# Window attention on one core: group-norm squares one per step, and 3x3 taps of the late strips shared out anew between VectorE, GpSimd and the routing

## The chip, the core and the metric

The kernel runs as one program on one core of one Trainium2 chip. The metric is the device time of one execution in microseconds. Before the change it was 12002.51 us, the median of three runs (11993.68 to 12006.19).

The core has five engines, each with its own instruction stream, which it works off in the order in which the program wrote it: TensorE (PE in the profile: matmuls and transposes into PSUM), VectorE (DVE), ScalarE (ACT), GpSimd (POOL), and SyncE (SP), which only issues transfers. They meet at semaphores: an instruction waits until what it reads has been written and what it overwrites has been read.

## The reference, cut to what matters

Four images of 256 channels and 64x64 pixels go through four layers; each is `x = x + layer(group_norm(x))`. Layers 0 and 1 are the ones the change is in: a two-way scan over the rows (computed by 1x1 convolutions, tanh, and a linear recurrence), then window attention with a 3x3 depthwise convolution of the values ("lepe") added to the attention's result. Layers 2 and 3 are state-space layers ("mamba"); they are not touched.

```python
def _gn(v, G=32, eps=1e-5):                  # one mean and variance per group of 2 columns
    m = jnp.mean(g, axis=(1, 2, 4), keepdims=True)
    s = jnp.var(g, axis=(1, 2, 4), keepdims=True)
    return ((g - m) / jnp.sqrt(s + eps)).reshape(v.shape)
...
def ssa(x_img, qkv_w, qkv_b, wo_w, wo_b, lepe_w, lepe_b):
    qkv = xw @ qkv_w.T + qkv_b               # 64 windows of 8x8 pixels
    logit = jnp.einsum('bpc,bqc->bpq', q_win * SCALE, k_win)
    tk_logit, idx = jax.lax.top_k(logit, TOPK)        # each window attends to 4 windows
    attn = jax.nn.softmax(jnp.einsum('bphqd,bphkd->bphqk', qh * SCALE, kh), axis=-1)
    out = jnp.einsum('bphqk,bphkd->bphqd', attn, vh)
    lepe = conv_general_dilated(v_img, lepe_w, (1, 1), 'SAME', feature_group_count=C) + lepe_b
    out_img = out_img + lepe
    return out_img @ wo_w.T + wo_b
```

## The kernel before, in words

An image stays in on-chip memory as `x`, 128 partitions by two channel halves by 4096 pixels. It is cut into 8 **strips** of 8 columns; a strip holds 4 groups of the group norm and one column of 8 windows. Per image the program does: attention layer 0, attention layer 1, then the two mamba layers. An attention layer has three stages.

**Scan stage** (`scan_phase`). One round per strip s: convolutions, the scan, and then `keys_values(s - 1)`, which makes keys and values of the strip before it (the values also as an image, `vimg`, line 357) and stores them in `kv_dram` for later gathers. Each round also runs the 3x3 taps of strip s-3 (`lepe`), so that strips 0 to 4 are done when the rounds end. After the last round comes `keys_values(7)`.

**Routing stage** (`routing` and the lines after its call). Means of queries and keys per window, logits, the four largest: a short chain that ends in the index list `idx`. Behind it stand the query convolutions of strips 2 to 4 on TensorE, evicted by VectorE, with the taps of strip 5 between them: channel half m=0 on VectorE, m=1 on GpSimd.

**Pair stage** (`window_phase`). 32 steps, i = 0 to 31, two windows each; strip sj = i // 4, and a = i % 4 is the place in the strip. A step is software pipelined with its neighbours and in two head halves h: scores on TensorE (line 538), their minimum on VectorE (`smallest`, line 550), exponentials with row sums on ScalarE (`exps`, line 561), a reciprocal on VectorE (line 573), four multiplications by it on GpSimd (`normalise`, line 576), transposes on TensorE (`turn`, line 589), copies out of PSUM by VectorE and ScalarE (`turned`, lines 600 and 602), products with the values (`values`, line 615), and the addition to `vimg` on VectorE (`own_rows`, line 626). Steps with a = 1 and 2 (from strip 1 on) also project the strip before (`project`: four 512-column matmuls, line 232, and an addition to `x` on VectorE, line 636). Steps 19, 20, 23 and 24 have a query convolution instead.

Every engine's order is written out by hand. Within a step there are two places where other work is hung in: **mids**, after the third and fourth exponential and ahead of `normalise(i, 0)`, and **ends**, after everything else of the step. A dictionary names for each step what goes there.

- **The taps.** A 3x3 convolution of one strip and channel half is nine taps. On VectorE a tap is one instruction (line 268 for the first, 270 for the others); in the scan and routing stages it accumulates in PSUM (`lp`), in the pair stage in `vimg` itself. On GpSimd the first tap is one instruction and each of the others two, `weigh` (line 253, into a scratch tile) and `add` (line 256): 17 pieces per half strip. The scratch tile has the tag "sq" of pool `norm`, with one buffer, and the group norm of the next layer (`gn`) takes the same tag for its squares. In the pair stage GpSimd has 51 pieces, one after each `normalise`, in steps 0 to 25: half m=1 of strip 6, then both halves of strip 7. VectorE has half m=0 of strip 6, one tap in each of steps 2 to 10.
- **Group norm for the next layer.** In layer 0's pair stage the strips 0 and 1 of `x` are normalised for layer 1 (`gn`): sums, a matmul that averages over partitions, `center` on GpSimd (line 151), a square on ScalarE (line 156), a reduction on VectorE (line 160), the matmul again, and `scale` on GpSimd (lines 168 and 172). In layer 1's pair stage all strips but the last get only their statistics for layer 2 (`stats`): sums on VectorE (line 200), the matmul (line 195), the mean (line 206), **squares**, four instructions on ScalarE in a row (line 215), the matmul, the variance (line 221). The two matmuls write the PSUM tile "mm", of which the pair stage has one, and which the convolutions use too.

What is left over when the 32 steps end (`left`) runs with the last projections.

Of the kernel before, what the change touches and what calls it, by code (L numbers as in the profile page):

```python
# [8 lines left out]
F32 = mybir.dt.float32  # L9
BF16 = mybir.dt.bfloat16  # L10
U32 = mybir.dt.uint32
AF = mybir.ActivationFunctionType
# [6 lines left out]
P = 128  # L19
NB = 4  # L20
C = 256
S = 64
T = S * S
NW = 8
# [20 lines left out]
class Net:  # L45
# [33 lines left out]
    def attention_layers(self, x, w_drams, v_drams):  # L79
        tc, nc = self.tc, self.nc  # L80
        with ExitStack() as ctx:
# [107 lines left out]
            def stats(s, psum):  # L189
                xs = x.rearrange("p (c h w) -> p c w h", c=2, w=S)[:, :, strip[s], :]  # L190
                box = {}
# [17 lines left out]

                def squares():  # L210
                    box["s2"] = self.small.tile([P, 4], F32, tag="gn_s2", name="gn_s2")
                    sq = norm.tile([P, 2, 8, S], F32, tag="xn", name="gn_sq")
                    for g in range(4):
                        two = slice(2 * g, 2 * g + 2)
                        nc.scalar.activation(
                            sq[:, :, two], xs[:, :, two], AF.Square,
                            bias=box["mean"][:, g : g + 1], accum_out=box["s2"][:, g : g + 1],
                        )

                def variance():  # L220
                    nc.vector.tensor_copy(self.gvar[:, 4 * s : 4 * s + 4], box["pv"][:, 0:4])

                return (
                    sums, lambda: columns("pm", box["s1"]), mean, squares,
                    lambda: columns("pv", box["s2"]), variance,
# [91 lines left out]
            def scan_phase(lay, work, psum, tail):  # L317
# [78 lines left out]
                for s in range(NW):  # L396
# [32 lines left out]
                    if s in (5, 6):  # L429
                        for evict in [query(lay, s - 5, m, psum) for m in range(2)]:  # L430
                            evict()
                keys_values(NW - 1)


# [33 lines left out]

            def window_phase(lay, work, psum, idx, nxt):
                vec, wb = lay["vec"], lay["wb"]  # L470
# [181 lines left out]
                smallest(0, 1)  # L652
                taps6, taps7 = (lepe(lay, s, pool=True) for s in (NW - 2, NW - 1))
                taps = taps6[17:] + taps7[17:] + taps7[:17]
                dve_taps = lepe(lay, NW - 2)[:9]

# [9 lines left out]
                if nxt:  # L666
                    load_scan_weights(nxt)
                    for s in range(2):
                        i = 10 + s
                        plan(gn(nxt, s, lambda: psum), (ends, i), (ends, i + 1), (mids, i + 2),  # L670
                             (ends, i + 2), (mids, i + 3), (ends, i + 5), (mids, i + 6))
                else:

                    for s in range(NW - 1):
                        i = 4 * s + 6
                        last = i + 6 if s < 5 else i + 3
                        plan(stats(s, lambda: psum), (ends, i), (ends, i + 1), (mids, i + 2),
                             (ends, i + 2), (ends, last), (mids, last + 1))
                for i in range(n_pair):
                    sj, a = divmod(i, 4)  # L680
# [14 lines left out]
                    normalise(i, 0)  # L695
                    for t in taps[2 * i : 2 * i + 1]:
                        t()
                    if a == 3 and sj + 2 in (NW - 2, NW - 1):
# [15 lines left out]
                    if i:  # L714
                        own_rows(i - 1)
                    for t in taps[2 * i + 1 : 2 * i + 2]:
                        t()
                    for t in dve_taps[i - 2 : i - 1] if i > 1 else ():
                        t()
                    if add:  # L720
# [36 lines left out]
            for i, lay in enumerate(layers):  # L757
                with tc.tile_pool(name=f"at_a{i}", bufs=1, reuse_waits="tile") as work, tc.tile_pool(
                    name=f"at_p{i}", bufs=5, space=PSUM, reuse_waits="tile"
                ) as psum:  # L760
                    box["psum"] = psum
                    scan_phase(lay, work, psum, tail)
                    idx = routing(lay, work, psum)
                    taps = lepe(lay, NW - 3, psum)[:9]
                    for s in range(2, 5):
                        evicts = [query(lay, s, m, psum, nc.vector) for m in range(2)]
                        for t in taps[3 * s - 6 : 3 * s - 3]:
                            t()
                        for evict in evicts:
                            evict()  # L770
                    for t in lepe(lay, NW - 3, pool=True)[17:]:
                        t()
                with tc.tile_pool(name=f"at_c{i}", bufs=1, reuse_waits="tile") as work, tc.tile_pool(
                    name=f"at_q{i}", bufs=1, space=PSUM, reuse_waits="tile"
                ) as psum:
                    nxt = layers[i + 1] if i + 1 < len(layers) else None
                    box, tail, left = window_phase(lay, work, psum, idx, nxt)
                    if nxt is None:
                        box["psum"] = psum
                        g = stats(NW - 1, lambda: psum)  # L780
                        for t in (left[0], tail[0], left[1], tail[1], g[0], left[2], left[3], *g[1:]):
                            t()
# [1381 lines left out]
```

## Time and profile before

| what | value |
|---|---|
| median of three runs | 12002.51 us |
| the profiled execution: its own time | 11985.03 us |
| its span, first to last instruction | 11983.3 us |
| PE, DVE, ACT, POOL busy | 84%, 82%, 58%, 74% of the span |
| pair stage, layer 0, first image: first exponential to last of step 31 | 234.6 to 487.5 us |
| pair stage, layer 1, first image | 701.2 to 954.1 us |
| granted TensorE clock, whole span | 0.932 |
| granted TensorE clock, the two pair stages | 0.92 and 0.91 |

The profile is one execution on the chip with the start and length of each instruction. A group row gives an engine, an operation, the tiles it writes and reads, how many there are, busy time, the mean length of one, and the idle time just before them with what ended it. A row of the timeline gives start, length, engine, line and operation; in square brackets stands how long the engine had been idle and who released it. A windows row gives, for a stretch of time, each engine's busy time and the share of its full clock that TensorE was granted. A step of the pair stage is measured here from its first exponential (line 561) to that of the next step; there are eight per step. There are eight pair stages, two per image, and the four images' stages differ little from each other: layer 0's last from 244.7 to 249.6 us and layer 1's from 246.4 to 248.6 us, first exponential of step 0 to first exponential of step 31.

### The profile page before, as it was taken

Reading aid. Unit: us, or ns where it says so; the run is one execution under the profiler, and the core shown is the slowest. Engines: PE = TensorE matmul, PEld = TensorE weight load, DVE = VectorE, ACT = ScalarE, POOL = GpSimd, SP = SyncE. Lnnn points to the kernel's source line nnn. Section 1 sums busy time; section 2 is a strip of 40 time slices with the busy share of each in tenths; the row PEclk is TensorE's granted clock in tenths of the full one; section 3 lists DMA queues with packets and bytes.
Section 4 is the critical chain, followed back from the end, with each engine's and each line's share of the span. In section 5 each row is a group of like instructions: output and inputs, shape, how many; then the busy total and the mean of one; then the engine's idle time right before and its main releaser. Section 6 shows DMA issues by size and latency. Waiting matters only on the chain.

```text
span 11983.3 us, 192241 instructions
## 1 busy us (share of the span) xinstructions
PE 10083.2 (84%) x71104; PEld 5778.2 (48%) x71104; DVE 9833.8 (82%) x8350; ACT 7002.3 (58%) x13096; POOL 8811.5 (74%) x6054
## 2 busy tenths in 40 slices
PE   8998887777899888777799988877778998887777
PEld 4564554444455455444445645544444554554444
DVE  6677998998666799899866779989986667998998
ACT  4555555776455555477645555547764555554776
POOL 4666886898456688689745668868984666887897
PEclk9999998999999899899999989989999999998999
DMA  3343454454334355445433434444543343454454
GB/s 96 100 126 134 174 175 149 169 180 160 92 98 127 134 173 177 145 169 182 159 90 99 128 132 173 174 148 167 180 160 91 100 127 135 173 176 146 169 176 154
DMA packets 682506, 1742.10 MB, mean 145 GB/s; under 512 B 88896, under 2 KB 194896, under 8 KB 681312
## 3 DMA queue, kind: packets, MB, share of 16 engines
q1 hardware_dynamic: 676448, 1721.41, 43.1%
q10 hardware_dynamic: 5120, 8.39, 0.3%
q8 instruction: 563, 9.22, 0.3%
q14 instruction: 375, 3.07, 0.1%
HBM read 1601.52 MB, written 94.39 MB: 142 GB/s over the span
## 4 chain that ended last, share of the span: by engine, by line
DVE 23%; PE 23%; ACT 8%; issue 5%; POOL 4%; DMA 1%; SPq 0%; DVEq 0%; POOLq 0%; ACTq 0%
DVE h L1002 13%; DVE pb L996 5%; PE conv_ps L232 4%; PE y L954 4%; PE u_ps L1291 3%; ACT da L938 2%; PE pb L926 1%; PE u_ps L1664 1%; POOL pr L576 1%; PE sc L538 1%; DVE lp L270 1%; PE pt_ps L589 1%; ACT dap L938 1%; PE z_ps L1316 1%; POOL hc L1008 1%
## 5 line engine op out<-in xcount | busy, mean ns | idle before, releaser
L1008 POOL TENSOR_TENSOR hc<-h,cb 128x1024 f32<-128x1024 f32 x2056 | 4809.6, 2350 | 806.4 <-DVE h L1002 350.9
L1002 DVE TENSOR_TENSOR_SCAN h<-da,m_state,pb 128x1024 f32<-128x1024 f32 x1248 | 2920.6, 2340 | 161.4 <-DVE pb L996 2.4
L954 PE MATMUL y<-ident,hc 128*128 128x128 f32 x16384 | 2333.6, 290 | 408.0 <-POOL hc L1008 340.9
L954 PEld LDWEIGHTS y<-ident,hc 128*128 128x128 f32 x16384 | 2034.5, 150 | 1124.9 <-POOL hc L1008 577.0
L996 DVE TENSOR_TENSOR pb<-du,pb 128x1024 f32<-128x1024 f32 x1672 | 2025.4, 1211 | 113.4 <-PE pb L926 110.9
L938 ACT ACTIVATE da<-delta,m_v 128x1024 f32<-128x1024 f32 x1672 | 1899.5, 1141 | 135.5 <-DVE h L1002 118.3
L926 PE MATMUL pb<-m_parts,pick 128*128 128x512 bf16 x3312 | 1078.2, 410 | 846.1 <-DVE h L1002 777.6
L576 POOL TENSOR_SCALAR pr<-pr,sm,zero 128x256 f32<-128x256 f32 x2048 | 1136.5, 569 | 476.8 <-DVE sm L573 475.8
L561 ACT ACTIVATE pr<-sc,mn 128x256 f32<-128x256 f32 x2048 | 955.9, 482 | 647.5 <-DVE sm L573 480.9
L926 PEld LDWEIGHTS <-pick 128*128 128x128 bf16 x3312 | 263.1, 101 | 1787.4 <-DVE h L1002 981.2
L550 DVE TENSOR_REDUCE mn<-sc 128x4 f32<-128x1024 f32 x512 | 627.9, 1228 | 550.0 <-PE sc L538 547.2
L1002 DVE TENSOR_TENSOR_SCAN h<-da,pb 128x1024 f32<-128x1024 f32 x424 | 969.5, 2287 | 55.1 <-DVE pb L996 0.9
L912 POOL TENSOR_TENSOR bb<-du,bb 128x1024 f32<-128x1024 f32 x376 | 888.6, 2363 | 88.8 <-DMA bb<-m_cd 84.0
L589 PE MATMUL pt_ps<-ident,pr 128*128 128x128 f32 x4096 | 705.4, 304 | 144.3 <-POOL pr L576 51.1
L1002 DVE TENSOR_TENSOR_SCAN h<-dap,m_state,bb 128x1024 f32<-128x1024 f32 x288 | 672.4, 2335 | 65.1 <-ACT dap L938 45.9
L232 PE MATMUL conv_ps<-att_y,att_wb 128*128 128x512 f32 x1536 | 683.3, 594 | 1.3 <-DVE gn_mean L206 1.3
L589 PEld LDWEIGHTS pt_ps<-ident,pr 128*128 128x128 f32 x4096 | 490.3, 151 | 307.5 <-POOL pr L576 161.7
L538 PE MATMUL sc<-kv,q_swap 32*64 32x128 f32 x8192 | 597.2, 287 | 6.7 <-DMA kv<-kv_dram 4.7
L938 ACT ACTIVATE dap<-delta,m_v 128x1024 f32<-128x1024 f32 x376 | 419.7, 1116 | 304.0 <-DVE h L1002 234.2
L538 PE MATMUL sc<-kv,att_y 32*64 32x128 f32 x7168 | 569.2, 287 | 11.8 <-DMA kv<-kv_dram 7.5
L538 PEld LDWEIGHTS sc<-kv,att_y 32*64 32x64 f32 x7168 | 430.0, 139 | 144.9 <-ACT pr L561 65.6
L270 DVE SCALAR_TENSOR_TENSOR lp<-vimg,att_v,lp 128x512 f32<-128x512 f32 x616 | 465.4, 756 | 28.1 <-DVE lp L270 1.4
(300 smaller groups left out, 17937.9 us busy)
## 6 DMA issues: line engine op xcount, KB each, us to landing
cb<-m_cd SPq DMA_DIRECT2D x2048, 512.0 KB, 3.8
kv<-kv_dram SPq DMA_DIRECT2D x1984, 128.0 KB, 2.8
bb<-m_cd SPq DMA_DIRECT2D x376, 512.0 KB, 5.4
kv_dram<-kst SPq DMA_DIRECT2D x128, 256.0 KB
kv_dram<-vn SPq DMA_DIRECT2D x128, 256.0 KB, 4.1
q_swap<-att_y SPq DMA_DIRECT2D x96, 256.0 KB, 4.3
m_pe<-in_pe_dram SPq DMA_DIRECT2D x32, 512.0 KB, 4.1
out_dram<-yo SPq DMA_DIRECT2D x64, 256.0 KB, 2.4
```

The lines of the kernel that those rows point to most:

```text
L232: nc.tensor.matmul(ps, w[:, k, w0 + m * P : w0 + (m + 1) * P], src[:, k], start=(k == 0), stop=(k == 1),)
L538: nc.tensor.matmul(sc[h][b * 64 : b * 64 + 64, r, w, m, :], (own(sj, m) if r == b else swap[sj % 2][:, m])[rows, 2 * a + w], kv[i, w][rows ...
L561: nc.scalar.activation(t[:, g].rearrange("p j r t -> p r j t"), sc[h][:, :, g // 2, g % 2, :].rearrange("p r (j t) -> p r j t", j=2), AF.E ...
L576: nc.gpsimd.tensor_scalar(t[:, g], t[:, g], s[:, g : g + 1], self.zero, ALU.mult, ALU.add)
L589: nc.tensor.transpose(pt[h][j][:, g, :], t[:, g, j].rearrange("p r t -> p (r t)"), self.ident,)
L912: nc.gpsimd.tensor_tensor(pb[i], slots[i][0]["du"], pb[i], ALU.mult)
L926: nc.tensor.matmul(pb[i][:, ss], self.pick[:, n : n + 1].to_broadcast([P, P]), blk["parts"][:, ss], start=True, stop=True,)
L938: nc.scalar.activation(da[i], blk["delta"], AF.Exp, scale=blk["a"](n))
L954: nc.tensor.matmul(blk["y"][:, ss], t[:, ss], self.ident, is_transpose=True, start=(n == 0 and ss.start % NT == 0), stop=(n == DS - 1 and ...
L996: nc.vector.tensor_tensor(pb[i], blk["du"], pb[i], ALU.mult)
L1002: nc.vector.tensor_tensor_scan(h[i][:, ss], da[i][:, ss], pb[i][:, ss], state, ALU.mult, ALU.add)
L1008: nc.gpsimd.tensor_tensor(hc[i][:, ss], h[i][:, ss], cb[i][:, ss], ALU.mult)
```

## The change

1. **Squares one by one.** `squares`, which issued four ScalarE instructions, becomes `square(g)`, which issues one; the plan puts them at four places.
2. **Other places in the plan.** In layer 1, `stats` of strip s starts at step i = 4s + 7 (before, 4s + 6): sums at the end of step i, matmul at the end of i+1, mean in the middle of i+2, the four squares at the end of i+2, middle of i+3, end of i+3, middle of i+4, the second matmul at the end of i+4, the variance in the middle of i+5. In layer 0, `gn` of strips 0 and 1 starts at steps 7 and 11 (before, 10 and 11): sums end of i, mean matmul end of i+1, `center` middle of i+2, square end of i+3, reduction middle of i+4, matmul end of i+4, `scale` middle of i+5.
3. **Taps of strip 5 ahead of `keys_values(7)`.** Half m=0 on VectorE (nine taps) and the first 5 of the 17 GpSimd pieces of half m=1 come before it, the other 12 pieces after it.
4. **Taps of strip 6 in the routing stage.** Half m=0 on VectorE between the queries, where strip 5 was, and 9 of the 17 GpSimd pieces of half m=1.
5. **Taps in the pair stage.** GpSimd has 25 pieces: 8 of strip 6 and the 17 of strip 7's half m=1, one at the end of each of steps 0 to 24. VectorE has half m=0 of strip 7, at the end of steps 3, 4, 7, 8, 11, 12, 15, 16 and 19.
6. **The last steps of layer 1** are reordered to match: the statistics of strip 6 now begin at step 31 and end among the last projections.

```diff
-                def squares():
-                    box["s2"] = self.small.tile([P, 4], F32, tag="gn_s2", name="gn_s2")
-                    sq = norm.tile([P, 2, 8, S], F32, tag="xn", name="gn_sq")
-                    for g in range(4):
-                        two = slice(2 * g, 2 * g + 2)
-                        nc.scalar.activation(
-                            sq[:, :, two], xs[:, :, two], AF.Square,
-                            bias=box["mean"][:, g : g + 1], accum_out=box["s2"][:, g : g + 1],
-                        )
+                def square(g):
+                    if g == 0:
+                        box["s2"] = self.small.tile([P, 4], F32, tag="gn_s2", name="gn_s2")
+                        box["sq"] = norm.tile([P, 2, 8, S], F32, tag="xn", name="gn_sq")
+                    two = slice(2 * g, 2 * g + 2)
+                    nc.scalar.activation(
+                        box["sq"][:, :, two], xs[:, :, two], AF.Square,
+                        bias=box["mean"][:, g : g + 1], accum_out=box["s2"][:, g : g + 1],
+                    )
...
                 return (
-                    sums, lambda: columns("pm", box["s1"]), mean, squares,
+                    sums, lambda: columns("pm", box["s1"]), mean,
+                    *(lambda g=g: square(g) for g in range(4)),
                     lambda: columns("pv", box["s2"]), variance,
                 )
...
+                for t in lepe(lay, NW - 3, psum)[:9]:
+                    t()
+                later = lepe(lay, NW - 3, pool=True)[17:]
+                for t in later[:5]:
+                    t()
                 keys_values(NW - 1)
+                for t in later[5:]:
+                    t()
...
-                taps6, taps7 = (lepe(lay, s, pool=True) for s in (NW - 2, NW - 1))
-                taps = taps6[17:] + taps7[17:] + taps7[:17]
-                dve_taps = lepe(lay, NW - 2)[:9]
+                taps = taps + lepe(lay, NW - 1, pool=True)[17:]
+                dve_taps = lepe(lay, NW - 1)[:9]
...
                     for s in range(2):
-                        i = 10 + s
+                        i = 7 + 4 * s
                         plan(gn(nxt, s, lambda: psum), (ends, i), (ends, i + 1), (mids, i + 2),
-                             (ends, i + 2), (mids, i + 3), (ends, i + 5), (mids, i + 6))
+                             (ends, i + 3), (mids, i + 4), (ends, i + 4), (mids, i + 5))
                 else:
 
                     for s in range(NW - 1):
-                        i = 4 * s + 6
-                        last = i + 6 if s < 5 else i + 3
+                        i = 4 * s + 7
                         plan(stats(s, lambda: psum), (ends, i), (ends, i + 1), (mids, i + 2),
-                             (ends, i + 2), (ends, last), (mids, last + 1))
+                             (ends, i + 2), (mids, i + 3), (ends, i + 3), (mids, i + 4),
+                             (ends, i + 4), (mids, i + 5))
...
                     normalise(i, 0)
-                    for t in taps[2 * i : 2 * i + 1]:
-                        t()
...
-                    for t in taps[2 * i + 1 : 2 * i + 2]:
+                    for t in taps[i : i + 1]:
                         t()
-                    for t in dve_taps[i - 2 : i - 1] if i > 1 else ():
-                        t()
+                    if a in (0, 3) and i and dve_taps:
+                        dve_taps.pop(0)()
...
                     idx = routing(lay, work, psum)
-                    taps = lepe(lay, NW - 3, psum)[:9]
+                    taps = lepe(lay, NW - 2, psum)[:9]
...
-                    for t in lepe(lay, NW - 3, pool=True)[17:]:
+                    later = lepe(lay, NW - 2, pool=True)[17:]
+                    for t in later[:9]:
                         t()
...
-                    box, tail, left = window_phase(lay, work, psum, idx, nxt)
+                    box, tail, left = window_phase(lay, work, psum, idx, nxt, later[9:])
                     if nxt is None:
                         box["psum"] = psum
                         g = stats(NW - 1, lambda: psum)
-                        for t in (left[0], tail[0], left[1], tail[1], g[0], left[2], left[3], *g[1:]):
+                        var, left = left[0], left[1:]
+                        for t in (var, tail[0], left[0], left[1], tail[1], *left[2:6], g[0],
+                                  left[6], left[7], *g[1:]):
                             t()
```

## The prediction, made before the changed kernel was run

> **What bounds the kernel now.** I read the page first, then windows of single steps and groups of steps, then timelines of ScalarE, GpSimd and VectorE in them.
>
> ```profile
> span 11983.3 us, 192241 instructions
> PE 10083.2 (84%) x71104; PEld 5778.2 (48%) x71104; DVE 9833.8 (82%) x8350; ACT 7002.3 (58%) x13096; POOL 8811.5 (74%) x6054
> DVE h L1002 13%; DVE pb L996 5%; PE conv_ps L232 4%; PE y L954 4%; PE u_ps L1291 3%; ACT da L938 2%; PE pb L926 1%; PE u_ps L1664 1%; POOL pr L576 1%; PE sc L538 1%; DVE lp L270 1%; PE pt_ps L589 1%; ACT dap L938 1%; PE z_ps L1316 1%; POOL hc L1008 1%
> ```
>
> No engine bounds the whole. Most of the chain (L1002, L996) is the mamba layers, which stay as they are. What can move is the eight pair stages, some 255 us each, 17% of the span. There the question is what a step costs with and without other work:
>
> ```profile
> 409.80:417.00 7.20, 7.06 (x151) 4.99 (x150) 4.15 (x9) 4.83 (x18) 6.22 (x10) 1.00 0.49 148
> 289.00:295.50 6.50, 5.50 (x139) 4.02 (x138) 6.03 (x8) 4.65 (x18) 5.51 (x10) 1.00 0.52 164
> 760.10:771.77 11.67, 11.67 (x187) 10.32 (x180) 6.09 (x12) 7.82 (x28) 9.11 (x14) 0.50 0.34 100
> 326.40:341.30 14.90, 12.82 (x228) 10.33 (x220) 7.92 (x13) 6.00 (x22) 12.72 (x17) 0.73 0.48 141
> 373.10:386.90 13.80, 11.40 (x166) 8.19 (x155) 4.49 (x10) 5.01 (x21) 12.80 (x16) 0.75 0.43 128
> ```
>
> Columns: length, busy time of PE, weight loads, DVE, ACT, POOL, then the granted clock. Row one is step 21, with a projection: TensorE is busy 7.06 of 7.20, it sets the step. Row two is step 7 of layer 0, without a projection but with a VectorE tap: 6.5. The other three are steps with group-norm work: step 8 of layer 1 (squares) and steps 12 and 17 of layer 0 (`center`, `scale`). They are 5 to 8 us longer and at a lower clock. What happens in them:
>
> ```profile
> 768.81 0.80 ACT L215 ACTIVATE gn_sq<-x,gn_mean 128x256 f32<-128x256 f32 x1
> 771.05 0.75 ACT L215 ACTIVATE gn_sq<-x,gn_mean 128x256 f32<-128x256 f32 x1
> ...
> 340.29 1.06 ACT L156 ACTIVATE gn_sq<-att_xn 128x1024 f32<-128x1024 f32 x1 [6.34 <-POOL vimg L256]
> ```
> ```profile
> 331.60 2.48 POOL L151 TENSOR_TENSOR att_xn<-x,gn_mean 128x1024 f32<-128x1024 f32 x1 [1.14 <-DVE sm L573]
> 334.05 2.17 POOL L576 TENSOR_SCALAR pr<-pr,sm,zero 128x256 f32<-128x256 f32 x4
> 336.19 0.77 POOL L253 TENSOR_SCALAR tap<-vimg,att_v,zero 128x512 f32<-128x512 f32 x1
> ```
>
> Layer 1: the first and last of four squares; from 768.81 to 771.8 ScalarE does nothing else, and the exponentials of step 9 stand behind it: 3.0 us. Layer 0: the square needs the scratch tile "sq", so it waits for the tap's `add` (L256) at the end of GpSimd's queue, itself behind `center`: ScalarE stands 6.34 us.
>
> **Part 1, squares one by one (layer 1).** In a step set by TensorE, ScalarE has two holes:
>
> ```profile
> 398.78 0.47 ACT L561 ACTIVATE pr<-sc,mn 128x256 f32<-128x256 f32 x1 [0.99 <-DVE sm L573]
> 409.82 0.47 ACT L561 ACTIVATE pr<-sc,mn 128x256 f32<-128x256 f32 x1 [1.14 <-DVE sm L573]
> ```
>
> 0.99 us at mids; 1.14 at ends, even behind a query eviction of 0.71. A square takes a place of 0.75, so each of the four fits and costs nothing; if the hole were gone it would cost 0.75. The block's 3.0 us per strip go. What comes instead: the mean (0.15, behind a 1.22 minimum) now stands ahead of the projection's matmuls, which need the one "mm" tile: TensorE waits about 0.5 (the variance did this in steps 13, 17, 21, 25, so there it is no news). Sums (1.22) stand at the end of steps with a = 3, behind a tap up to step 19, and delay `turned` by 0.8; before, they stood behind tap and addition. From step 23 on nothing is lost: own rows and sums are 0.4 + 1.22, as much as own rows and an addition (0.4 + 1.36).
>
> Layer 1, by groups of four steps (first image). After: a = 1 7.7 (with the mean), a = 2 7.3, a = 3 6.6 (6.9 with the second matmul), a = 0 7.4 (6.6 and the sums' 0.8):
> - steps 5 to 8: 35.8 now; 7.2 + 7.2 + 6.6 + 7.4 = 28.4
> - 9 to 12: 32.8; 7.7 + 7.3 + 6.9 + 7.4 = 29.3
> - 13 to 16: 33.3; 29.3
> - 17 to 20: 30.9; two query steps, 7.7 + 7.3 + 7.5 + 8.4 = 30.9
> - 21 to 24: 30.9; 7.7 + 7.3 + 7.3 + 7.9 = 30.2
> - 25 to 28: 30.9; 7.7 + 7.3 + 6.8 + 7.0 = 28.8
> - 29 and 30: 17.0; 7.7 + 7.3 = 15.0
>
> 211.6 becomes 191.9, less 19.7. The tail pays: sums of strip 6 in the last step (half hidden, +0.6) and its matmul between the two last projections (+0.6): net 18.5 per image.
>
> **Part 2, the norm of layer 0.** `center` (2.48) is still ahead of `normalise(i, 0)`; a transpose needs that 1.1 us after it ends (GpSimd's multiplications end at 401.03 in step 19, its transposes start about 402.2), less with the tap gone, so it costs 1.7 (bounds 1.4 and 2.5). `scale` is 1.65 + 1.90 by the trace, less the same 1.1: 2.5. The square stands at the end of steps 10 and 14, where the piece before it is again an `add` (pieces 9 to 24 alternate). That `add` waits for `normalise(i, 1)`, whose reciprocal comes late: in the trace step 19 starts at 395.38 and step 18's multiplications run to 397.65, so the `add` would end at 398.8, 3.4 us after the next step's exponentials are due. Cost 3.4, between 2 (GpSimd ahead) and 4.5 (the square's own 1.06 added), plus 1.0 for clock: 4.4. Layer 0, steps 4 to 19: 136.8 now. After: 4 and 7 at 6.6; 5, 6, 10, 14, 17, 18 at 7.3; 8 at 7.4; 9 and 13 at 9.0; 11 and 15 at 11.0; 12 at 9.9 (with the second sums); 16 at 9.1; 19 at 7.5. Sum 130.9, less 5.9. Steps 1 to 3 wait for the first gathers and stay.
>
> **Part 3, taps moved ahead of and around the routing.** The hole they go into:
>
> ```profile
> 217.81 0.69 DVE L389 COPY vn<-vt_ps 128x512 f32<-128x512 f32 x1 [7.10 <-PE vt_ps L383]
> 212.99 0.67 POOL L361 COPY vst<-vimg 128x512 f32<-128x512 f32 x1 [5.12 <-ACT vimg L357]
> 238.37 2.16 POOL L576 TENSOR_SCALAR pr<-pr,sm,zero 128x256 f32<-128x256 f32 x4 [5.36 <-DVE sm L573]
> ```
>
> VectorE is idle 7.10 us before the last `vn` copy; the round before, nine PSUM taps ran from 184.47 to 191.67, 7.2. The copy comes 0.1 late; ScalarE's half of `vn` ends later still (218.84), so nothing follows. GpSimd is idle 5.12: five pieces are 0.77 + 2 x 2.13 (start to start in a lone row of pieces) = 5.0. The other 12 (12.8) and 9 of strip 6 (9.3) start at 215.3 and end at 237.4; `normalise(0, 0)` starts at 238.37 (0.5 us of room in layer 1). Cost 0, cover gone: 1 us per layer. The half strip that changes engine is 16.4 us of GpSimd pieces against 7.2 of VectorE.
>
> [...] Row: taps that accumulate in `vimg` took 969 ns (median), in PSUM 756 ns, also beside GpSimd pieces. [...] The nine pair-stage taps are as many as before.
>
> **Part 4, fewer pieces in the pair stage.** GpSimd loses 26 of 51 pieces, some 25 us per layer, but where TensorE sets the step that is idle time. It pays in steps 5, 6, 9, 10 (8.7, 7.9, 8.4, 7.9 in layer 0, to 7.3), which is in the sums above. No transfer and no ScalarE or SyncE queue entry moves; GpSimd issues none.
>
> **Sum.** 18.5 + 5.9 = 24.4 per image, 97.6 in four. The profiled execution took 11985.03 (span plus 1.7); less 97.6 is 11887. The median stands 17.5 above it, so I predict **11905**.
>
> [...] In the pair stages 8% and 9% of the clock is missing, 20 to 23 us each if all were on the path; I book none of it as gain beyond the sums.
>
> **Rivals.**
> - *More* (0.14): the clock stays full once the blocks are gone and the square waits are short; layer 1 gives 24, layer 0 14: 38 per image, 11850. For it: groups 17 to 24 already run at 1.00.
> - *Less* (0.16): steps without a projection are held by their hand-offs, not by squares; each square shifts a minimum or a transpose. Layer 1 gives 9, layer 0 nothing: 11966.
> - *No change* (0.04): the saved time turns into waits for gathers. Against it: gathers are issued three steps ahead, TensorE waits for `kv` before step 4 and then only at step 28, under 0.7 us.
> - *Slower* (0.06), by the clock: where one long stall per strip shut the gate once, small gaps in three steps shut it three times. A 3.4 us window at half clock costs 1.7; the pair stages lose (1 - clock) x 255. To eat the 24.4 per image the clock must fall by 0.05 in both, to 0.87 and 0.86; at 0.85, about 12035. Against it: step 7, full of 1 us gaps, at 1.00.
> - The forecast's own case: 0.60.
>
> **Numbers.** A difference under 0.2% (24 us) can't be told from none in this kernel. Faster by more: 0.60 + 0.14 + nearly all of "less" = 0.88; within: 0.06; slower: 0.06. The range 11845 to 11980 goes from most of "more" to most of "less".
>
> **What would show it.** Right: no ScalarE row L215 directly behind another in the stage; steps of layer 1 with a = 0 at 6.6 to 8.4; the wait of L156 for L256 at 3 to 4 us, not 6.4; idle before the last `vn` copy near 0; granted clock in layer 1's stage over 0.93. Wrong: exponentials waiting after lone squares, `normalise(0, 0)` behind a tap, clock at or under 0.87, or VectorE idle ahead of PE in steps 7, 11, 15, 19.

## The result, and the profile after

The changed kernel takes **11905.7 us** (median of 4 runs, 11900.46 to 11917.89) beside 12000.29 us for the kernel before on the same chip: a ratio of 0.9925, 95% interval 0.9911 to 0.9939. The forecast was 11905. The total was met, but by luck: two of the terms in it were wrong by 23 us each, in opposite directions, and the reason given for the largest gain covers less than half of it.

From the page of the changed kernel, its span and busy shares:

```profile
span 11901.3 us, 192225 instructions
PE 10069.9 (85%) x71104; PEld 5762.7 (48%) x71104; DVE 9868.8 (83%) x8422; ACT 7006.9 (59%) x13096; POOL 8695.6 (73%) x5918
```

Still no engine bounds the whole. GpSimd has 136 instructions fewer and VectorE 72 more: the half strip of taps that changed engine. The steps shown before (21, 7, 12 and 17 of layer 0, 8 of layer 1), and step 13 of layer 0 behind 12, by windows (length, busy time of PE, weight loads, DVE, ACT, POOL, then the granted clock):

```profile
410.88:418.09 7.21, 7.08 (x151) 5.00 (x149) 4.17 (x8) 4.84 (x19) 5.47 (x9) 1.00 0.47 149
287.28:292.97 5.69, 5.05 (x141) 3.97 (x140) 5.19 (x7) 4.70 (x18) 5.07 (x9) 1.00 0.63 177
756.00:762.85 6.85, 6.02 (x158) 4.60 (x148) 6.12 (x9) 4.84 (x21) 5.89 (x9) 1.00 0.57 159
325.71:332.97 7.26, 6.78 (x165) 5.92 (x158) 6.13 (x10) 4.81 (x18) 5.42 (x7) 0.83 0.52 147
332.97:348.02 15.05, 12.62 (x170) 8.68 (x159) 5.74 (x11) 4.97 (x21) 11.94 (x15) 0.66 0.38 107
375.31:388.81 13.50, 12.79 (x172) 8.30 (x165) 5.02 (x9) 4.94 (x18) 8.01 (x13) 0.60 0.39 120
234.30:489.80 255.50, 232.31 (x4523) 170.97 (x4525) 161.08 (x251) 158.00 (x579) 177.50 (x286) 0.88 0.50 143
703.30:928.50 225.20, 213.22 (x4531) 156.21 (x4533) 162.25 (x260) 173.23 (x624) 165.75 (x280) 0.98 0.56 158
```

Step 8 of layer 1 fell from 11.67 at clock 0.50 to 6.85 at 1.00. Layer 0's long step did not go away, it moved: 12 is short now, 13 takes 15.05, and 17 is as long as before (13.80 then) at a clock of 0.60. The last two rows are the first image's whole pair stages, 252.9 each before: layer 1's is 27.7 shorter, layer 0's 2.6 longer.

Over the four images of the profiled executions, from the first exponential of step 0 to that of step 31: layer 1 went from 990.1 to 896.3 us (-93.8), layer 0 from 987.2 to 987.4, the stretch behind layer 1's last step from 104.5 to 101.7, the stretch between the two pair stages (norm, scan, routing of layer 1) from 876.3 to 875.2. The rest, most of it the mamba layers that the change does not touch, took 15.8 us more in this execution (8790.6 to 8806.4). It lies between 8802.6 and 8819.5 in the profiles of all the kernels below; the profiled execution of the kernel before was the odd one, as the 17 us by which it lies under its own median say.

### The profile page after: what moved, and what is told of

It is laid out like the page before. It is cut to its first block, busy times and chain, and to the rows that moved or that the text cites. A ratio compares the mean times of both kernels' runs of the same rounds, so it can differ in the third digit from the quotient of the medians.

```text
span 11901.3 us, 192225 instructions
## 1 busy us (share of the span) xinstructions
PE 10069.9 (85%) x71104; PEld 5762.7 (48%) x71104; DVE 9868.8 (83%) x8422; ACT 7006.9 (59%) x13096; POOL 8695.6 (73%) x5918
## 5 line engine op out<-in xcount | busy, mean ns | idle before, releaser
L597 PE MATMUL pt_ps<-ident,pr 128*128 128x128 f32 x4096 | 663.9, 297 | 85.0 <-POOL pr L584 40.2
L271 DVE SCALAR_TENSOR_TENSOR lp<-vimg,att_v,lp 128x512 f32<-128x512 f32 x672 | 507.7, 755 | 30.8 <-DVE lp L271 1.0
```

Source lines behind the costliest of these rows:

```text
L597: nc.tensor.transpose(pt[h][j][:, g, :], t[:, g, j].rearrange("p r t -> p (r t)"), self.ident,)
```

## The experiments

Each ratio below is to the kernel before, run on the same chip. The groups of runs stood on different chips, on which the kernel before took 11994 to 12004 us; two rows are therefore compared by their ratios. The columns "layer 1" and "layer 0" are the mean over four images of the time from step 0 to step 31, from one profile each; "half" adds up, over four images, the whole stretches at a granted clock of 0.50 that begin in the pair stages.

| kernel | median us | ratio, 95% interval | layer 1 | layer 0 | half, layer 1 | half, layer 0 |
|---|---|---|---|---|---|---|
| before | 12000.3 | 1 | 247.5 | 246.8 | 194.6 | 177.5 |
| changed | 11905.7 | 0.9925 (0.9911 to 0.9939) | 224.1 | 246.9 | 61.4 | 208.2 |
| squares_block | 11915.1 | 0.9932 (0.9915 to 0.9948) | 226.2 | 247.1 | 61.4 | 211.6 |
| plan_only | 11898.2 | 0.9918 (0.9902 to 0.9935) | 224.4 | 245.7 | 58.0 | 184.3 |
| own_tap_tile | 11860.5 | 0.9884 (0.9867 to 0.9900) | 226.9 | 234.9 | 85.3 | 112.6 |
| split_scale | 11872.1 | 0.9902 (0.9885 to 0.9918) | 224.6 | 238.0 | 64.9 | 146.8 |
| spread_only | 11966.3 | 0.9978 (0.9970 to 0.9986) | 236.7 | 244.8 | 139.9 | 150.2 |
| block_late | 11979.8 | 0.9988 (0.9979 to 0.9996) | 240.0 | 245.9 | 146.8 | 157.0 |
| sums_late | 11911.4 | 0.9920 (0.9903 to 0.9937) | 226.9 | 246.3 | 37.5 | 163.8 |
| tile_and_split | 11826.7 | 0.9859 (0.9842 to 0.9875) | 223.6 | 227.3 | 54.6 | 64.9 |
| sums_twice_apart | 11955.3 | 0.9968 (0.9958 to 0.9978) | 233.7 | 244.4 | 133.1 | 187.7 |
| sums_twice_together | 11945.2 | 0.9953 (0.9936 to 0.9969) | 235.5 | 244.9 | 126.3 | 204.8 |
| plan_and_repairs | 11861.6 | 0.9886 (0.9870 to 0.9903) | 224.0 | 235.4 | 44.4 | 71.7 |

How far to trust the layer columns: layer 1 has the same plan in the changed kernel, own_tap_tile, split_scale and tile_and_split, and measures 223.6 to 226.9; layer 0 has the same in the changed kernel, squares_block and the two sums_twice kernels, and measures 244.4 to 247.1. A difference under 3 us per image between two of these profiles is therefore not read as an effect unless single steps show it.

### Layer 1: is it the squares?

**squares_block**: the changed kernel with its four squares back in one block.

```diff
-                    *(lambda g=g: square(g) for g in range(4)),
+                    lambda: [square(g) for g in range(4)],
+                    lambda: None, lambda: None, lambda: None,
```

> The changed kernel with one thing undone: the four squares of a strip again in a row at the end of step i+2, all else as changed. My theory (each square fits a hole of ScalarE, the block does not): layer 1 loses 3.0 us at each of the six blocks in the stage (steps 9, 13, ... 29) and some clock, about 18 us per image, so about 11975 us; layer 0 does not move. Rival (the gain of layer 1 comes from the taps that left GpSimd and from the other places of the sums, the squares do not matter): under 10 us in all, about 11910.

Measured: layer 1 +2.1 us per image, too little to be told from nothing, against the 18 or so that the block would have cost by the prediction's account. Steps with a = 1 grow by about 0.8 (17 from 8.25 to 8.97) and those with a = 2 shrink from 7.21 to 6.84. The block as such is nearly free at its new place, the end of steps with a = 1, so something else that the change did to layer 1 brought the gain. Compared with the kernel before, three things are different: where the sums stand, where the squares stand, and whether these are spread. (The taps are not it: plan_only, below, has layer 1 at 224.4 without their move.) The three were then taken apart on the kernel before, as far as that goes: the squares need the mean and the mean the sums, so later sums take the block with them.

**spread_only**: the squares over four places (ends of a = 0, mids and ends of a = 1, mids of a = 2), the sums where they were.

```diff
-                             (ends, i + 2), (ends, last), (mids, last + 1))
+                             (ends, i + 2), (mids, i + 3), (ends, i + 3),
+                             (mids, i + 4) if s < 5 else (ends, i + 3),
+                             (ends, last), (mids, last + 1))
```

> The kernel before, with its four squares of a strip spread over four places and everything else where it was (the sums still at the end of a step with a = 2, behind the addition). The prediction's account (each strip loses a 3.0 us block that held up the exponentials): layer 1 loses some 3 us in each of steps 8, 12, 16, 20, 24 and 28, about 15 us per image, 60 in all: 11935. The account formed after the block came back for 2.1 us per image (the gain of layer 1 is that of the sums' place, not of the spreading): step 7 keeps its stall and the half clock that it sets off, layer 1 loses 3 to 7 us per image: 11965 to 11985.

**block_late**: the block whole, one step later.

```diff
-                             (ends, i + 2), (ends, last), (mids, last + 1))
+                             (ends, i + 3), (ends, last), (mids, last + 1))
```

> The kernel before, with the block of four squares whole, but moved from the end of steps with a = 0 to the end of steps with a = 1; nothing else changes. If the place of the block is what made it dear (3 us of ScalarE ahead of a step that already starts late): layer 1 loses 12 to 18 us per image, 11925 to 11950. If the sums' place is what counts: under 5 us per image, 11975 to 11995, with half clock still beginning in steps 7 and 11.

**sums_late**: sums, mean and squares one step later, the squares still a block. The second matmul and the variance of strips 0 to 4 come one step earlier than in the kernel before, right behind the squares.

```diff
-                        i = 4 * s + 6
+                        i = 4 * s + 7
...
-                             (ends, i + 2), (ends, last), (mids, last + 1))
+                             (ends, i + 2), (ends, i + 4), (mids, i + 5))
```

> The kernel before, with every piece of a strip's statistics one step later (the sums at the end of steps with a = 3, where no addition stands ahead of them), the squares still in one block. If the sums' place makes the gain: layer 1 loses about 20 us per image, 11905 to 11920, and no half clock begins in step 7. If place and spreading share it evenly, some 10 us per image: 11950.

Measured: spreading alone gives 10.8 us per image of layer 1, the later block 7.5, the later start, which has the later block in it, 20.7, all of the change 23.4. In time, sums_late has 84.8 of the 94.6 us. The times of spread_only and block_late lie where the account by the sums' place had them; their traces show some 3 us per image more than it allowed, but the profiled executions were the fastest of their runs, 10.5 and 12.2 us under the medians, which would be 3 per image.

Why the place of the sums matters is seen on VectorE. In the kernel before, at the end of step 6 (a = 2), first image:

```profile
752.52 0.97 DVE L270 SCALAR_TENSOR_TENSOR vimg<-vimg,att_v 128x512 f32<-128x512 f32 x1
753.41 1.34 DVE L636 SCALAR_TENSOR_TENSOR x<-conv_ps,att_v,x 128x512 f32<-128x512 f32 x1
754.79 1.22 DVE L200 TENSOR_REDUCE gn_s<-x 128x4 f32<-128x1024 f32 x1
755.93 0.68 DVE L600 COPY pts<-pt_ps 128x512 f32<-128x512 f32 x1
```

And TensorE, in the same kernel, waiting for that copy:

```profile
755.04 0.33 PE L589 MATMUL pt_ps<-ident,pr 128*128 128x128 f32 x1 [0.21 <-POOL pr L576]
756.66 0.66 PE L589 MATMUL pt_ps<-ident,pr 128*128 128x128 f32 x4 [1.29 <-DVE pts L600]
```

Tap, addition and sums stand in one queue ahead of the copy (L600) that empties the PSUM tile for TensorE's next transposes. TensorE stands 1.29 us at 755.4, and at 758.6 the clock goes to 0.50 for 13.65 us; all of step 8 runs in it (the row 760.10:771.77 shown in the prediction). In sums_late the same copy comes right behind the addition, and one step later the sums stand without one:

```profile
752.34 1.35 DVE L636 SCALAR_TENSOR_TENSOR x<-conv_ps,att_v,x 128x512 f32<-128x512 f32 x1
753.58 0.70 DVE L600 COPY pts<-pt_ps 128x512 f32<-128x512 f32 x1
...
758.43 1.04 DVE L270 SCALAR_TENSOR_TENSOR vimg<-vimg,att_v 128x512 f32<-128x512 f32 x1
759.39 1.21 DVE L200 TENSOR_REDUCE gn_s<-x 128x4 f32<-128x1024 f32 x1
760.52 0.68 DVE L600 COPY pts<-pt_ps 128x512 f32<-128x512 f32 x1
```

Steps 7 and 8 of sums_late by windows:

```profile
751.23:757.79 6.56, 5.56 (x141) 4.08 (x140) 6.06 (x8) 4.71 (x18) 5.55 (x10) 1.00 0.58 158
757.79:764.75 6.96, 6.13 (x160) 4.63 (x148) 6.19 (x9) 4.88 (x20) 6.71 (x11) 1.00 0.56 169
```

6.56 and 6.96 at full clock, where the kernel before had 7.8 and 11.66. Its TensorE has no gap over 0.62 us here. Over four images half clock begins in step 7 four times in the kernel before, in spread_only and in block_late, and once in sums_late.

The block in its old place has a wait of its own. ScalarE's copy out of PSUM (L602) stands behind it and two exponentials. TensorE in step 13 of the kernel before, and at the same place behind the block in step 14 of block_late:

```profile
806.14 0.91 PE L589 MATMUL pt_ps<-ident,pr 128*128 128x128 f32 x4 [1.17 <-ACT pts L602]
```
```profile
811.56 0.63 PE L589 MATMUL pt_ps<-ident,pr 128*128 128x128 f32 x4 [0.73 <-ACT pts L602]
```

The gap of 1.17 us is there in all four images, and half clock follows it in all four; behind the later block the gap is 0.73 to 0.75 and none follows. So half clock follows two different places of the old plan. By the step in which it begins: sums at the end of steps with a = 2, the old place, come just before a = 3; the block at the end of a = 0 before a = 1; sums at the end of a = 3, the new place, before a = 0. Stretches at half clock that begin in steps 5 to 30 of layer 1, in four images, with their length together in us:

| kernel | begin in a = 3 | begin in a = 1 | begin in a = 0 |
|---|---|---|---|
| before | 15 (102.4) | 9 (30.7) | 0 |
| spread_only | 12 (78.5) | 0 | 0 |
| block_late | 14 (92.2) | 0 | 0 |
| sums_late | 1 (3.4) | 0 | 1 (3.4) |
| changed | 4 (23.9) | 0 | 0 |
| sums_twice_apart | 14 (88.7) | 0 | 0 |
| sums_twice_together | 1 (3.4) | 0 | 15 (71.7) |

Before and block_late have one more each in a = 2 (3.4). The last two rows are the next runs.

**sums_twice_apart** and **sums_twice_together** put the queue back on purpose: the changed kernel with a second, idle reduction of 1.22 us, once behind the addition at a = 2, once directly ahead of the sums at a = 3.

```diff
-                    sums, lambda: columns("pm", box["s1"]), mean,
+                    sums, sums, lambda: columns("pm", box["s1"]), mean,
...
-                        plan(stats(s, lambda: psum), (ends, i), (ends, i + 1), (mids, i + 2),
+                        plan(stats(s, lambda: psum), (ends, i - 1), (ends, i), (ends, i + 1), (mids, i + 2),
```

The second kernel has `(ends, i), (ends, i)` in that place.

> The changed kernel, with each strip's sums made twice: once more at the end of the step with a = 2, behind the addition (1.22 us, its result overwritten), then again where they are. If it is the queue of addition and sums on VectorE, ahead of the copies that TensorE's next transposes wait for, that shuts the clock gate: the gap of 1.3 us in step 7 and the half clock after it are back, layer 1 gains nothing over before, 15 to 22 us per image come back: 11965 to 11995. If the sums' old place was bad for another reason (the pieces that follow them came one step earlier), only the reduction's own time shows: at most 1.22 us for each of seven strips, 8.5 per image: 11940.

> The changed kernel, with each strip's sums made twice in a row at the end of the step with a = 3 (2.44 us where addition and sums were 2.57). If the length of VectorE's queue ahead of those copies is what counts, in whichever step, a gap over 1.2 us and half clock come in step 8 and 12, 10 to 20 us per image: 11945 to 11985. If the step (a = 2) or the addition itself is what counts: at most 1.22 us for each strip, 8.5 per image: 11940 or less, without half clock.

In turn: TensorE's wait for the copy in sums_twice_apart, the windows of its steps 7 and 8, TensorE's wait in sums_twice_together, and the window of its step 8:

```profile
746.83 0.66 PE L597 MATMUL pt_ps<-ident,pr 128*128 128x128 f32 x4 [0.84 <-DVE pts L608]
```
```profile
743.34:750.29 6.95, 5.46 (x119) 4.09 (x120) 6.42 (x8) 4.71 (x18) 5.11 (x9) 0.88 0.51 149
750.29:760.28 9.99, 9.99 (x172) 8.50 (x164) 6.22 (x10) 4.98 (x20) 5.93 (x9) 0.50 0.45 135
```
```profile
757.78 0.66 PE L597 MATMUL pt_ps<-ident,pr 128*128 128x128 f32 x4 [1.02 <-DVE pts L608]
```
```profile
753.27:761.25 7.98, 6.25 (x136) 4.64 (x128) 7.24 (x10) 4.85 (x21) 5.93 (x9) 0.89 0.61 176
```

The half clock is back, in the steps where the reduction was put: it begins in step 7 four times in the first kernel, in steps 8, 12 and 16 three, four and four times in the second, and "half" rises from 61 to 133 and 126. So one more reduction in VectorE's queue ahead of the copies brings it back, in either step; neither the addition nor the step a = 2 is needed for it. The gaps in the lines above are 0.84 and 1.02 us, less than the 1.3 and "over 1.2" that were expected.

The price was lower than expected too: 9.6 and 11.5 us per image between step 0 and step 31, where six of the seven added reductions fall; their own time is 7.3 (6 x 1.22). The half clock is thus shown, but what it costs beyond the reductions' own time, 2 to 4 us, is not resolved. The apart kernel falls between its two expectations, the together one at the low end of the first. Part of the price is plain delay: in step 23, which stays at full clock, the reduction costs 1.05.

What the kernel before lost in layer 1, 23.4 per image, can be split in two ways. By spread_only: 10.8 by the block at its old place, 12.6 by the rest. By block_late and sums_late: 7.5 by the block's old place, 13.1 by the places of the sums and of what hangs on them, 2.8 (not told from nothing) by the block being whole and by the taps. Either way somewhat more than half goes with the sums and less than half with the block, and of the block's part most goes when it is moved whole. How much of the 13 is the sums and how much the mean, the second matmul and the variance was not taken apart; that the sums' queue sets off the half clock is what the sums_twice kernels show.

### Layer 0: which wait, which price?

**own_tap_tile**: the changed kernel, with the taps' partial sums in a scratch tile of their own, so that the square of the norm shares nothing with them.

```diff
-                        both = norm.tile([P, 2, 8, S], F32, tag="sq", name="tap", bufs=1)
-                        box[m] = both[:, m]
+                        box[m] = norm.tile([P, 8, S], F32, tag="tap", name="tap", bufs=1)
```

> The changed kernel, but GpSimd's taps have a scratch tile of their own, so that layer 0's square no longer waits for the last add. My theory: steps 10 and 14 of layer 0 fall from 11.7 to about 7.3 us, 8.8 us per image, about 11870 us. Rival (GpSimd is late in any case, and what the square gives up the next reciprocal or transpose waits for): steps 11 and 15 grow by as much, 11900.

The square on ScalarE in the changed kernel, and then in own_tap_tile:

```profile
318.85 1.06 ACT L156 ACTIVATE gn_sq<-att_xn 128x1024 f32<-128x1024 f32 x1 [4.89 <-POOL vimg L257]
```
```profile
311.54 1.07 ACT L156 ACTIVATE gn_sq<-att_xn 128x1024 f32<-128x1024 f32 x1
```

A wait of 4.89 has become none. Steps 10 and 14 fall from 11.75 and 11.61 to 7.37 and 7.23, by 4.38 each; steps 11 and 15 grow by 1.0 and 0.4, not by as much as the rival had it. Layer 0 falls by 12.0 per image: 7.3 in these four steps, 2.0 in step 16, the rest scattered.

**split_scale**: the multiplication by the standard deviation's inverse one place behind the power.

```diff
+                    box["rstd"] = rstd
+
+                def spread():
                     xn = lay["xn"][s]
-                    nc.gpsimd.tensor_tensor(xn, xn, wide(rstd), ALU.mult)
+                    nc.gpsimd.tensor_tensor(xn, xn, wide(box["rstd"]), ALU.mult)
...
-                             (ends, i + 3), (mids, i + 4), (ends, i + 4), (mids, i + 5))
+                             (ends, i + 3), (mids, i + 4), (ends, i + 4), (mids, i + 5),
+                             (ends, i + 5))
```

> The changed kernel, but layer 0's scale is cut in two: the power (1.65 us) stays in the middle of steps 12 and 16, the multiplication (1.90 us) moves to the end of the same steps. My theory now (the clock): scale makes TensorE stand 2.2 us and then run some 10 us at half clock, so it costs 8 us; two delays of under 2 us, partly inside the 1.1 us of room, keep the clock up: steps 12 to 13 and 16 to 17 fall from 22.4 to about 17 us each, 10 us per image, about 11862 us. Rival (GpSimd's work itself): 3.55 us of work ahead of a normalise costs the same in two pieces: within 5 us of 11905.

GpSimd in the changed kernel, then in split_scale:

```profile
330.81 1.64 POOL L168 TENSOR_TENSOR gn_rstd<-gn_rstd,minus_half 128x8 f32<-128x8 f32 x1 [1.61 <-DVE sm L581]
332.53 1.90 POOL L172 TENSOR_TENSOR att_xn<-att_xn,gn_rstd 128x1024 f32<-128x1024 f32 x1
334.42 4.74 POOL L584 TENSOR_SCALAR pr<-pr,sm,zero 128x256 f32<-128x256 f32 x8
```
```profile
329.29 1.65 POOL L168 TENSOR_TENSOR gn_rstd<-gn_rstd,minus_half 128x8 f32<-128x8 f32 x1 [1.29 <-DVE sm L584]
330.93 4.76 POOL L587 TENSOR_SCALAR pr<-pr,sm,zero 128x256 f32<-128x256 f32 x8
335.65 1.19 POOL L260 TENSOR_TENSOR vimg<-vimg,tap 128x512 f32<-128x512 f32 x1
336.80 1.90 POOL L175 TENSOR_TENSOR att_xn<-att_xn,gn_rstd 128x1024 f32<-128x1024 f32 x1
```

What the first order does to TensorE of the changed kernel:

```profile
335.46 2.94 PE L597 MATMUL pt_ps<-ident,pr 128*128 128x128 f32 x8 [2.24 <-POOL pr L584]
340.47 1.97 PE L597 MATMUL pt_ps<-ident,pr 128*128 128x128 f32 x8
342.23 3.37 PE L233 MATMUL conv_ps<-vimg,att_wb 128*128 128x512 f32 x4
```

Power and multiplication together hold the eight multiplications of `normalise`, and TensorE stands 2.24 us. From 334.98 the clock is at 0.50 for 10.24 us: eight transposes take 1.97 where eight take 1.09 at full clock (at 347.59). With the two apart, steps 12 and 13 together fall from 22.45 to 18.35, 16 and 17 from 22.45 to 17.92, and layer 0 by 8.9 per image.

**tile_and_split**: both repairs.

> The changed kernel with both repairs: the taps' partial sums in a tile of their own (so that the square waits for no tap), and the norm's multiplication one place behind its power. If the two costs are separate, they add: 11905.7 less 45.3 and 33.6 is 11827. If each repair mostly took away the same half clock, less than their sum: 11845 to 11855.

11826.73. The ratios, which leave out the difference between the chips, say the same: 0.9925 less 0.0041 and 0.0023 is 0.9861, and 0.9859 (0.9842 to 0.9875) was measured. That the two times agree to 0.3 us is chance. The two costs are separate, and this is the fastest kernel of the study: 1.4% under the kernel before, nearly twice the gain of the change.

### The taps

**plan_only**: the changed kernel's places for squares and norm, with all taps as the kernel before has them (51 pieces, two in each step).

> The kernel before with parts 1, 2 and 6 alone: squares one by one and the new places in the plan, the taps where they were (51 pieces on GpSimd in the pair stage, strip 5 after the routing). My theory: layer 1 keeps the squares' gain of some 16 to 18 us per image and lacks the taps' 5 to 7; layer 0 is as before or up to 4 us per image slower, since the square still waits for an add and GpSimd is fuller: about 11945 us. Rival (the taps carry the gain): 11990 or more.

The taps' move brings nothing measurable: 0.9918 without it, 0.9925 with it. In layer 1 the changed kernel is 4.2 us ahead by step 11 (5, 6 and 10 are 0.6 to 0.7 shorter), and gives 3.6 of it back by step 20. Its VectorE taps stand ahead of the sums in the steps up to 19, which fits; it was not tested.

**plan_and_repairs**: plan_only with both repairs.

> The changed kernel's plan with the taps where the kernel before has them, and both repairs (own tile for the taps' sums, the norm's multiplication one place later). If the taps' move is worth nothing also without the two waits: 11898.2 less 45.3 and 33.6 is 11819. If the pieces of GpSimd now stand ahead of center and of the multiplication where the repairs had taken that wait away: 11840 or more.

Here the move does count: 11861.6 without it, 11826.7 with it, by the ratios 0.0027 (give or take 0.0023) of 12000, 32 us. All of it is in layer 0, 8.0 per image: 0.7 in steps 5, 6, 17 and 18 each, 1.4 in step 10, 2.9 in step 14. GpSimd and TensorE around step 14, in plan_and_repairs:

```profile
338.60 2.46 POOL L151 TENSOR_TENSOR att_xn<-x,gn_mean 128x1024 f32<-128x1024 f32 x1
341.06 2.17 POOL L579 TENSOR_SCALAR pr<-pr,sm,zero 128x256 f32<-128x256 f32 x4
```
```profile
341.66 0.33 PE L592 MATMUL pt_ps<-ident,pr 128*128 128x128 f32 x1 [1.44 <-POOL pr L579]
```

In tile_and_split the same transposes waited less:

```profile
337.06 0.33 PE L599 MATMUL pt_ps<-ident,pr 128*128 128x128 f32 x1 [0.73 <-POOL pr L586]
```

1.44 against 0.73; half clock begins in step 14 in four images of four, against two. A reading of this, not tested: while each strip lost 4.4 to the square and several us to the multiplication, GpSimd caught up with its pieces in that time, and fewer of them gained nothing.

## Why the prediction held, and where it did not, step by step

- **Sum.** 97.6 us were booked: 74 in layer 1 (18.5 per image with its tail), 23.6 in layer 0. The traces show 96.6 in layer 1 and its tail, and nothing in layer 0. Errors of +22.6 and -23.8 cancelled; that the total came out within 1 us is luck. The 17.5 us added for the distance of the profiled execution from the median was right: the untouched stretches show it.
- **Layer 1, the levels of the steps after.** Steps 5 to 30 were booked at 191.9 and measure 190.9, group by group within 1.2. These levels were read off steps without group-norm work, so they hold whatever had kept the other steps from them. The gain that was not booked is elsewhere: 1.0 since the mean of four images was 212.6 and not the first image's 211.6, 1.7 in steps 0 to 4, and a tail that costs -0.7 instead of +1.2.
- **Layer 1, the cause. This step failed**: "The block's 3.0 us per strip go" was to bring the whole gain, with the sums' new place booked only as a cost of 0.8. The runs show the block at 10.8 of the 23.4 (spread_only), and 12.6 that come with the new places. In the steps behind the sums' old queue half clock began 15 times in four images, against 4 after the change. The prediction's own words named the queue ("before, they stood behind tap and addition") and did not price it. Nor was it the block's 3.0 us of ScalarE: whole, one step later, it gives back 7.5 of the 10.8, and whole in the changed kernel it costs 2.1, not 18. What it held up in its old place was a copy that TensorE waited for, 1.17 us and the half clock behind that.
- **Layer 0, square: right.** Booked 4.4 in steps 10 and 14, so 18.3 with the step behind each; 17.7 and 17.5 measured, and 4.38 each when the shared tile went. The wait itself was 4.89 and 4.83, longer than the 3 to 4 named as its sign. No run shows the 1.0 for clock in the 4.4 by itself: the 4.38 of own_tap_tile is wait and clock together.
- **Layer 0, `center`: a little dear.** Step 9 is 8.44, booked 9.0: 1.1 and not 1.7.
- **Layer 0, `scale`: this term failed.** It was booked at 2.5, its 3.55 on GpSimd less the slack of 1.1, and no clock on top. Steps 12 and 13 were booked at 18.9 and measure 22.45, 16 and 17 at 16.4 and measure 22.45: 9.6 per image, more than the 7.9 by which layer 0 missed; charged to `scale` alone, that makes 6.0 and 8.5 a time. Cut in two it gave back 4.1 and 4.5 of these; the rest was not traced. The price stood in the row 373.10:386.90 (13.80 at clock 0.75) of the kernel before, a step with the same order of GpSimd's work. A slack subtraction sees the gap and not the half clock behind it; for the square a clock term was booked, here it was forgotten.
- **Routing: right.** The nine taps cost nothing. The last `vn` copy of the changed kernel starts directly behind the ninth:

```profile
216.92 0.75 DVE L271 SCALAR_TENSOR_TENSOR vimg<-vimg,att_v,lp 128x512 f32<-128x512 f32 x1
217.66 0.69 DVE L390 COPY vn<-vt_ps 128x512 f32<-128x512 f32 x1
```

  The nine take 7.2 us from the first to the copy, beside GpSimd's pieces, as much as in the round before, and `normalise(0, 0)` starts at 238.11, 1.1 behind the last piece. The row in the prediction held: a tap in PSUM took 756 ns (median) in both kernels, one into `vimg` 969 before and 964 after.
- **Fewer pieces: half right.** Step 5 was to fall to 7.3 and fell to 8.06 and 7.87 in the two layers, step 6 to 7.37 and 7.21. The gain was real, but other waits of the same layer took it up until the repairs had removed them.
- **The clock.** Step 8 of layer 1 was at 0.50 in the kernel before, with no gap of TensorE over 1.3 us ahead of it (1.29, at 755.4); how much idle time half clock followed in the traces stands below. To book "none of it as gain beyond the sums" was too careful for layer 1 and too generous for layer 0: its mean over the four images, weighed by time, went from 0.91 to 0.97 in layer 1 and from 0.91 to 0.89 in layer 0. Of the rivals, "more" was right for layer 1 alone (24 booked there, 24.1 measured with the tail), "less" for layer 0.
- **Signs.** No square directly behind another, steps with a = 0 at 6.6 to 7.7 from step 8 on, but for the query step 20 (8.57), layer 1's clock over 0.93, no idle time before the last `vn` copy: all there. The square's wait alone was longer than its sign.

## What to carry to other kernels

Ahead of any claim that a long block is what costs, look at the queue in front of the short copy that frees TensorE's PSUM tile. Here it was two or three VectorE instructions of about a microsecond each in a row at one place and ScalarE's block of squares at another, and the same block one step later cost 2 us per image or nothing. When a wait of an almost full TensorE is priced, price the gap and the half clock behind it (at `scale` 2.24 us and 10.24 us at 0.50), from a row that already shows both. And when an edit shows no gain, undo it again after the larger waits are gone: the taps' move went from nothing to 32 us.

## What the hardware showed that was not expected

In the traces of before and of the changed kernel, all stretches at half clock in the pair stages begin on one fixed grid of 3.41 us and last a whole number of its periods, one (3.41) to eight (27.3). Counted over the windows of this grid in steps 2 to 30 of both kernels that were at full clock themselves, by the time in which TensorE had no matmul:

| TensorE idle in the window, us of 3.41 | windows | next window at half clock |
|---|---|---|
| under 0.7 | 792 | 3 |
| 0.7 to 1.0 | 23 | 6 |
| 1.0 to 1.3 | 33 | 18 |
| 1.3 and more | 45 | 45 |

So about one microsecond of idle in 3.41 was even odds here, and 1.3 was followed by half clock every time, in one gap or in several: seven of the windows in the last row have no gap over 0.7. That is the size of one queued reduction (1.22). Why the same step differs between images (in the kernel before, the half clock that begins in step 7 of layer 1 lasts 13.65 us in two images and 3.41 in the two others) may be where the gap falls on the grid; that was not tried. The ends of matmuls are modelled in the trace, so the edges of the classes are rough.
